# The first group of x loaded in two halves on two queues, and seven early products instead of nine

## The chip, the cores and the metric

The kernel runs on one core of one Trainium2 chip. The metric is device time in microseconds. Three runs of the kernel before gave 664.02, 663.25 and 662.78 us; the median is 663.25 us. The engines are TensorE (PE, with its weight loads as PEld), VectorE (DVE), ScalarE (ACT), GpSimd (POOL) and SyncE (SP). Transfers can be issued by SyncE, ScalarE and GpSimd, each with a queue of its own.

## The reference

Input x is (4, 2048, 256), all in 32-bit floats. Two layers follow one another, each with a residual sum and a layer norm after it:

```python
# attention without softmax, causal
q, k, v = (gelu(x @ W1 + b1) @ W2 + b2  for each of q, k, v)
scores = (q @ k.T) / sqrt(256 * 512) * tril(ones)
x = layernorm(x + (layernorm(scores @ v) * ln_w + ln_b))
# mixture of experts with soft slots: 16 experts of 16 slots
xn = layernorm(x) * gamma + beta
logits = unit(xn) * scale @ unit(mu)
dispatch, combine = softmax(logits over tokens), softmax(logits over slots)
slot_in = dispatch.T @ xn
slot_out = gelu(slot_in @ w1 + b1) @ w2 + b2        # per expert
x = layernorm(x + combine @ slot_out)
```

## The kernel before

**Tiling.** A group is W = 512 tokens (G = 4 blocks of 128 partitions by 256 channels); there are 16 groups, four to a batch element. For each group the kernel transposes x to channels by tokens (`xT`), makes the hidden layers of q, k and v (128x512 products with W1q, W1k, W1v at L802, each followed by ScalarE's Gelu at L812), and then k and v, the causal part, a running state, the norms and the logits. W2q and W2k are folded into one matrix at the start (`fold`, L728 on): both are transposed on TensorE (L738), copied by VectorE (L746), multiplied with one another (L760) and written by VectorE to `wqk_sb` (L770). The output of these three products goes through the three PSUM banks called `mm`, which the products of q, k and v use as well.

**Order.** Work is entered as steps with an engine, a length and what they read and write. A planner (`Plan`) lists the steps for each engine by expected times and ranks, and emits them in that order; each engine then runs its instructions in the order of emission. The framework adds semaphores for what depends on what, part by part of a tile. Loading is a step of the engine "SP" in the plan, whatever queue its transfers go to.

**Loading.** `load_x(t)` (L308) loads group t with one transfer of 512 KB on SyncE's queue (L315). For the first group it then calls `load_weights` (L370), which puts W1q, cols (the bias columns, 9 KB), W1v and W2q on ScalarE's queue in this order, W1k, W2k and W2v on SyncE's (256 KB each; L375 and L377), and mu, scale and two vectors on GpSimd's. After the second group's x comes `rows` (L387), 640 KB. Groups 0 and 1 are transposed on TensorE from x as loaded: `flips` (L479) puts four 128x128 transposes of one half of the channels into a bank (L486), first for half 0, then for half 1; `transpose_group` copies the first bank on VectorE (L476) and the second on ScalarE (L477). From group 2 on, x is loaded a second time as blocks of 32 by 32 in eight transfers of 64 KB (L338), which VectorE transposes in place (L787). For group 2 this comes on VectorE between the copies of the transposed W2q and W2k (L746) and those of the folded products (L770).

**Early products.** Before any data is there, TensorE multiplies the identity with itself (L461), nine times; each 32-bit product is two instructions in the profile. The results are not used.

Of the kernel before, what the change touches and what calls it, by code (L numbers as in the profile page):

```python
# [14 lines left out]
P = 128  # L15
G = 4
# [10 lines left out]
W = G * P  # L27
# [192 lines left out]
def kernel(  # L220
# [13 lines left out]
    nc = tc.nc  # L234
    B, T, C = x.shape
    E, _, H = w1.shape
# [71 lines left out]
    def load_x(t):  # L308
        if t >= ngroups:
            return  # L310
        b, g = divmod(t, NG)
        xt = plan.buffer("row", G)

        def emit():
            nc.sync.dma_start(  # L315
                out=xt[:, :, :C],
                in_=x[b, g * W : (g + 1) * W, :].rearrange("(c p) d -> p c d", p=P),
            )
            if t == 0:
                load_weights()  # L320
            if t == 1:
                load_rows()

        plan.step("SP", {0: 2.5, 1: 6.0, 2: 4.0}.get(t, 0.5), emit, writes=[xt])
        x_tiles[t] = xt
        if t < 2:
            return


        xs = plan.buffer("xT", KC)  # L330

        def emit_blocks():
            xb = x[b, g * W : (g + 1) * W, :].rearrange(
                "(n c) (k a r) -> a c k n r", c=32, k=KC, r=32
            )
            for a in range(P // 32):
                for k in range(KC):
                    nc.sync.dma_start(  # L338
                        out=xs[32 * a : 32 * (a + 1), k, :].rearrange(
                            "c (n r) -> c n r", r=32  # L340
                        ),
                        in_=xb[a][:, k],
                    )

        plan.step("SP", 4.8, emit_blocks, writes=[xs])
        xs_tiles[t] = xs
# [23 lines left out]
    def load_weights():  # L370
        for n, eng in (
            ("W1q", nc.scalar), ("W1k", nc.sync), ("W1v", nc.scalar),
            ("W2k", nc.sync), ("W2q", nc.scalar), ("W2v", nc.sync),
        ):
            eng.dma_start(out=wa[n], in_=w_attn[n].rearrange("(k p) d -> p k d", p=P))  # L375
            if n == "W1q":
                nc.scalar.dma_start(out=cols_sb, in_=cols)  # L377
        nc.gpsimd.dma_start(out=mu_sb, in_=mu.rearrange("(k p) e -> p k e", p=P))
        nc.gpsimd.dma_start(out=scale_sb, in_=scale.partition_broadcast(P))
        with nc.allow_non_contiguous_dma(reason="two vectors of one value a partition"):  # L380
            nc.gpsimd.dma_start(
                out=gb_sb.rearrange("p r k -> p (r k)"),
                in_=rows[3 * C : 5 * C].rearrange("(q p) -> p q", p=P),
            )

    def load_rows():
        nc.sync.dma_start(  # L387
            out=rows_sb.rearrange("p r d -> p (r d)"), in_=rows.partition_broadcast(P)
        )
# [31 lines left out]
    for n, after in (  # L421
# [29 lines left out]
        out=mask,  # L451
        in_=ones,
# [4 lines left out]
        channel_multiplier=-1,  # L457
    )

    for _ in range(9):  # L460
        nc.tensor.matmul(at_banks[0][:, :P], ident, ident, start=True, stop=True)  # L461

    hz_t = const.tile([P, NP, 2, S], F32, name="hz")
# [1106 lines left out]
    for t in range(ngroups):  # L1570
        b = t // NG
# [11 lines left out]
        if t == ngroups - 2:  # L1583
# [4 lines left out]
            cm, _ = softmaxes(early)  # L1588
            plan.begin(t + TAIL["part"])
            kept = part_sums(early)  # L1590
        if t % NG == NG - 1:
            groups = [t] if tail == 2 else list(range(t - NG + 1, t + 1))
            plan.begin(t + (TAIL["soft"] if tail == 2 else 1.4))
            _, less = softmaxes(groups, cm if tail == 2 else None)
# [52 lines left out]
```

## Time and profile before

| | us |
|---|---|
| median of the runs | 663.25 |
| the profiled execution | 663.13 |
| its span | 661.4 |
| TensorE busy | 647.2 (98%) |
| VectorE busy | 490.9 (74%) |
| GpSimd busy | 298.5 (45%) |
| ScalarE busy | 266.1 (40%) |
| first early product starts | 1.42 |
| first transpose of x starts | 5.64 |
| first product of q starts | 7.54 |
| first transpose of W2q starts | 11.08 |
| first product of v starts | 18.83 |

The page's first lines give each engine's busy time, its share of the span and its number of instructions. The chain of waits is followed back from the last instruction: each line has a start, a length, and what ran. A timeline line has start, length, engine, line, operation, and what it writes and reads; in brackets stands how long the engine stood idle before it and what ended that. "SPq" and "ACTq" are transfers issued by SyncE and ScalarE. In the lines on transfers, q1 is SyncE's queue, q10 ScalarE's and q0 GpSimd's, with packets, megabytes and the share of 16 transfer engines. The granted clock is 1.00 in all stretches up to 600 us.

### The profile page before, as it was taken

What the parts mean: (1) busy time and instruction counts of PE and PEld (TensorE: products, weight loads), DVE (VectorE), ACT (ScalarE), POOL (GpSimd) and SP (SyncE); (2) the same over time, 40 slices, a digit from 0 to 9 for tenths busy, and PEclk for the clock granted to TensorE, in tenths of its full rate; (3) what the DMA queues carried; (4) which work ended last, traced back from release to release, by engine and by line L of the source; (5) the groups of instructions that cost most, each with busy time, mean ns of one, the idle gap of its engine ahead of it and who ended that gap; (6) DMA issues with size and microseconds to landing.
All of it is one profiled execution on the core that took longest, in us unless ns stands there. A gap on an engine that the chain in (4) does not pass through costs nothing.

```text
span 661.4 us, 9366 instructions
## 1 busy us (share of the span) xinstructions
PE 647.2 (98%) x2972; PEld 483.3 (73%) x2972; DVE 490.9 (74%) x1294; ACT 266.1 (40%) x597; POOL 298.5 (45%) x346
## 2 busy tenths in 40 slices
PE   9999999999999999999999999999999999999995
PEld 6657586777768877758686887776767768887874
DVE  1438586979797878778796388996978489886486
ACT  3130515333346227221516323634153544545475
POOL 4343616060739514353426605546061937646234
PEclk9999999999999999999999999999999999999998
DMA  8953655777577095836676525994677372621274
GB/s 247 261 123 109 129 96 130 126 152 158 99 158 128 15 199 174 188 87 128 127 130 136 87 68 91 238 212 104 109 152 133 65 160 70 83 65 32 33 160 160
DMA packets 322233, 84.71 MB, mean 128 GB/s; under 512 B 253068, under 2 KB 319944, under 8 KB 322184
## 3 DMA queue, kind: packets, MB, share of 16 engines
q1 hardware_dynamic: 321080, 83.06, 59.7%
q10 hardware_dynamic: 960, 0.80, 0.4%
q8 instruction: 23, 0.38, 0.2%
q0 software_dynamic: 144, 0.26, 0.1%
q14 instruction: 26, 0.21, 0.1%
HBM read 52.05 MB, written 32.04 MB: 127 GB/s over the span
## 4 chain that ended last, share of the span: by engine, by line
PE 92%; DVE 5%; issue 1%; POOL 1%; POOLq 0%; ACT 0%; DVEq 0%; ACTq 0%
PE mm L802 25%; PE at L904 8%; PE mm L1171 8%; PE mm L852 8%; PE at L1316 8%; PE at L1542 7%; PE at L987 7%; PE mm L825 7%; PE at L877 4%; PE at L991 4%; PE at L937 1%; PE at L461 1%; PE tp L486 1%; DVE xn L1096 1%; PE mm L683 1%
## 5 line engine op out<-in xcount | busy, mean ns | idle before, releaser
L812 ACT ACTIVATE hid<-mm,cols_sb 128x512 f32<-128x512 f32 x96 | 65.1, 686 | 142.1 <-PE mm L802 141.5
L542 POOL TENSOR_TENSOR root<-ve,nhalf 128x4 f32<-128x4 f32 (+1 forms) x39 | 40.7, 1044 | 125.1 <-DVE ve L1037 51.2
L987 PE MATMUL at<-state,hid 128*128 128x256 f32 x240 | 61.6, 379 | 0.0
L904 PE MATMUL at<-vt,kt 128*128 128x256 f32 x240 | 61.3, 385 | 0.0
L825 PE MATMUL mm<-both_sb,hid 128*128 128x257 f32 x256 | 59.5, 381 | 1.4 <-DVE kt L835 1.4
L802 PE MATMUL mm<-xT,W1v_sb 128*128 128x512 f32 x128 | 59.5, 593 | 0.7 <-DVE both_sb L770 0.7
L802 PE MATMUL mm<-xT,W1q_sb 128*128 128x512 f32 x128 | 59.5, 595 | 0.3 <-DVE xT L476 0.3
L1542 PE MATMUL at<-so,ct 128*128 128x256 f32 x256 | 57.9, 381 | 0.8 <-DVE row L1550 0.6
L1316 PE MATMUL at<-row,lg 128*128 128x257 f32 x256 | 58.2, 380 | 0.0
L1171 PE MATMUL mm<-mu_sb,xnT 128*128 128x256 f32 x256 | 58.1, 379 | 0.0
L852 PE MATMUL mm<-W2v_sb,hid 128*128 128x256 f32 x256 | 58.0, 379 | 0.0
L802 PE MATMUL mm<-xT,W1k_sb 128*128 128x512 f32 x128 | 57.7, 593 | 0.0
L825 PEld LDWEIGHTS mm<-both_sb,hid 128*128 128x128 f32 x256 | 48.2, 190 | 9.7 <-DVE kt L835 2.0
L1542 PEld LDWEIGHTS at<-so,ct 128*128 128x128 f32 x256 | 48.0, 190 | 9.9 <-issue 1.7
L1171 PEld LDWEIGHTS mm<-mu_sb,xnT 128*128 128x128 f32 x256 | 48.4, 190 | 8.4 <-issue 1.5
L987 PEld LDWEIGHTS at<-state,hid 128*128 128x128 f32 x240 | 45.6, 190 | 11.8 <-issue 5.7
L1030 POOL TENSOR_TENSOR row<-row,rows_sb 128x1024 f32<-128x1024 f32 x16 | 35.0, 2186 | 42.4 <-DMA row<-in_x_dram 33.9
L852 PEld LDWEIGHTS mm<-W2v_sb,hid 128*128 128x128 f32 x256 | 48.5, 190 | 6.7
L1221 POOL TENSOR_TENSOR sum<-sum,ss 128x4 f32<-128x4 f32 x16 | 4.0, 248 | 109.4 <-DVE ss L1217 92.9
L1316 PEld LDWEIGHTS at<-row,lg 128*128 128x128 f32 x256 | 48.1, 190 | 7.2 <-issue 0.4
L904 PEld LDWEIGHTS at<-vt,kt 128*128 128x128 f32 x240 | 44.4, 190 | 12.0 <-issue 5.4
L946 ACT COPY cs<-at 128x256 f32<-128x256 f32 (+1 forms) x16 | 5.9, 371 | 109.1 <-PE at L937 97.5
(150 smaller groups left out, 1250.8 us busy)
## 6 DMA issues: line engine op xcount, KB each, us to landing
bounce<-xn SPq DMA_DIRECT2D x30, 512.0 KB
row<-in_x_dram SPq DMA_DIRECT2D x16, 512.0 KB
ct<-bounce SPq DMA_DIRECT2D x64, 128.0 KB
bounce<-kt SPq DMA_DIRECT2D x30, 256.0 KB
kT<-bounce SPq DMA_DIRECT2D x60, 128.0 KB
out_dram<-row SPq DMA_DIRECT2D x15, 512.0 KB
xT<-in_x_dram SPq DMA_DIRECT2D x112, 64.0 KB
xnT<-bounce SPq DMA_DIRECT2D x56, 128.0 KB
```

Source lines behind the costliest of these rows:

```text
L542: nc.gpsimd.tensor_tensor(r[:, :n], v[:, :n], nhalf.to_broadcast([P, n]), ALU.pow)
L802: nc.tensor.matmul(ph.place, wa[f"W1{n}"][:, k, m * P : (m + 1) * P], xT[:, k, :], start=(k == 0), stop=(k == KC - 1),)
L812: nc.scalar.activation(hid[n][:, m, :], ph.place, AF.Gelu, bias=cols_sb[:, 4 * i + m : 4 * i + m + 1],)
L825: nc.tensor.matmul(pk[:, : C + 1], hid["k"][:, k, c * P : (c + 1) * P], wqk_sb[:, k, :], start=(k == 0), stop=(k == KC - 1),)
L852: nc.tensor.matmul(pv[:, j * C : (j + 1) * C], hid["v"][:, k, (c0 + j) * P : (c0 + j + 1) * P], wa["W2v"][:, k, :], start=(k == 0), stop=( ...
L877: nc.tensor.matmul(psc[:, toks[c]], kT[:, k, toks[c]], qT[:, k, toks[c]], start=(k == 0), stop=(k == KC - 1),)
L904: nc.tensor.matmul(pds[:, m * C : (m + 1) * C], kt[:, c, m * P : (m + 1) * P], vt[:, c, :], start=True, stop=True,)
L987: nc.tensor.matmul(po[:, :C], qT[:, k, toks[c]], s[:, k, :], start=(k == 0), stop=False,)
L1030: lambda: nc.gpsimd.tensor_tensor(row[:, :, :C], row[:, :, :C], lnb_r, ALU.add),
L1171: nc.tensor.matmul(pl[:, j * ES : (j + 1) * ES], xnT[:, k, (c0 + j) * P : (c0 + j + 1) * P], mu_sb[:, k, :], start=(k == 0), stop=(k == KC ...
L1316: nc.tensor.matmul(psi[:, : C + 1], lg[:, c, h * P : (h + 1) * P], row[:, c, :], start=(i == 0), stop=(i == n - 1),)
L1542: nc.tensor.matmul(pc[:, :C], ct[:, h, c * P : (c + 1) * P], so_t[:, h, :], start=(h == 0), stop=(h == EH - 1),)
```

## The change

For the first group only, the load of x is two transfers of 256 KB: blocks 0 and 1 on SyncE's queue, blocks 2 and 3 on ScalarE's, both issued before the weights, so that W1q is second on ScalarE's queue. All other groups are loaded as before. Seven early products are issued instead of nine.

```diff
         def emit():
-            nc.sync.dma_start(
-                out=xt[:, :, :C],
-                in_=x[b, g * W : (g + 1) * W, :].rearrange("(c p) d -> p c d", p=P),
-            )
+
+            for i, eng in enumerate((nc.sync, nc.scalar) if t == 0 else (nc.sync,)):
+                n = G // 2 if t == 0 else G
+                cs = slice(i * n, (i + 1) * n)
+                eng.dma_start(
+                    out=xt[:, cs, :C],
+                    in_=x[b, g * W : (g + 1) * W, :].rearrange("(c p) d -> p c d", p=P)[:, cs],
+                )
             if t == 0:
                 load_weights()
...
-    for _ in range(9):
+    for _ in range(7):
         nc.tensor.matmul(at_banks[0][:, :P], ident, ident, start=True, stop=True)
```

## The prediction

> **What bounds the kernel now.** I read the page first, then the chain of waits for the first 40 us, because the change touches nothing later, then the timeline and the transfers of the first 20 us.
>
> ```profile
> span 661.4 us, 9366 instructions
> ...
> PE 647.2 (98%) x2972; PEld 483.3 (73%) x2972; DVE 490.9 (74%) x1294; ACT 266.1 (40%) x597; POOL 298.5 (45%) x346
> ```
>
> TensorE (PE) is busy 98% of the span, so only its few idle places can be won or lost. The chain of the start (start us, length us, what):
>
> ```profile
> 1.42 4.21 PE at L461 x18
> ...
> 5.64 1.92 PE tp L486 x8
> 7.56 3.69 PE mm L802 x8
> 11.24 0.87 PE tp L738 x8
> 12.12 3.43 PE mm L802 x8
> 15.55 2.62 PE mm L760 x12
> ...
> 18.39 0.40 DVE both_sb L770
> ...
> 18.83 3.70 PE mm L802 x8
> ```
>
> Nine early products are 18 instructions (L461). Then come x's transposes (L486), the q products (L802), the transposes of W2q and W2k (L738), the k products, and the folded weight (L760). Up to 18.2 us the chain is TensorE alone; then, for one step, it is VectorE (DVE). The timeline shows what each step stood waiting for:
>
> ```profile
> 5.33 0.37 SPq L315 DMA_DIRECT2D row<-in_x_dram  x1
> 5.64 1.57 PEld L486 LDWEIGHTS tp<-ident,row 128*128 128x128 f32 x8 [0.31 <-DMA row<-in_x_dram]
> ...
> 5.74 0.54 SPq L387 DMA_DIRECT2D rows_sb<-in_rows_dram  x1
> ...
> 10.97 0.91 PEld L738 LDWEIGHTS tp<-ident,both_sb 128*128 128x128 f32 x8 [0.56 <-DMA both_sb<-in_W2q_dram]
> ...
> 17.22 1.25 DVE L787 STREAM_TRANSPOSE xT<-xT 128x1024 f32<-128x1024 f32 x1 [4.14 <-DMA xT<-in_x_dram]
> ...
> 18.39 1.05 DVE L770 TENSOR_SCALAR both_sb<-mm 128x257 f32<-128x257 f32 x3
> ...
> 18.83 1.55 PE L802 MATMUL mm<-xT,W1v_sb 128*128 128x512 f32 x3 [0.67 <-DVE both_sb L770]
> ```
>
> Three waits matter. x lands just as the early products end (5.6 us). W2q lands at 10.93 us by its semaphore events, and its first weight load goes out at 10.97, so W2q is just in time. And DVE stands at L787 until the third group's xT has landed (17.14 us); only then does it empty the first folded bank (L770), whose bank the v products need. TensorE waits 0.67 us for that. Transfers up to 4.75 us (packets, MB):
>
> ```profile
> q1 hardware_dynamic: 444, 0.45, 29.0%
> q10 hardware_dynamic: 266, 0.26, 21.4%
> ```
>
> q1 is SyncE's queue (x first), q10 is ScalarE's (W1q first). Both are in flight together, and ScalarE's first 256 KB (256 packets) are through by about 4.8 us.
>
> **The change, part by part.**
>
> *Two early products fewer.* Each is two instructions, 18 in 4.21 us, 0.213 us apart. Four of them are 0.85 us; TensorE is free at 4.78 instead of 5.63 us, and could take a transpose at 4.57. Whether that is worth anything hangs on x.
>
> *x in halves.* SyncE's half is 256 packets. q1 had sent its 256th at 3.8 us and its 512th at 4.93; x's semaphore was full at 5.60. The half should be seen by about 4.5. ScalarE's half stands where W1q stood: W1q's 256 packets were out at 4.8 and it was seen at 5.31. So I take 5.31 for it (not before 4.9, if q10 starts sooner behind a shorter x; not after 5.60). Halves of a tile are waited for one by one: the q products start on xT's first half at 7.54 and take the second at 8.23, "0.39 <-ACT xT L477". So two transposes run before 5.31; the third and fourth end at 5.97, DVE's copy (0.69 us, L476) ends at 6.7, and the q products could start at 6.73 instead of 7.54.
>
> *W1q second on its queue.* From 4.85 us both queues share about 365 GB/s, as from 4.5 to 5.5 us now. Half of it takes 1.4 us for 256 KB, plus the 0.5 us from W1q's last packet to its semaphore now: 6.75 to 6.95 us. The q products then start at about 6.85, 0.7 us sooner, and end at 10.4.
>
> *W2q, last on ScalarE's queue.* It now stands behind 256 KB more. After W1q come cols (a gap of 0.35 us and 0.45 us of small packets, as now), so W1v starts at about 7.05 instead of 5.9 us: some 165 packets behind by what q10 moved in that time. Late in the queue (9 to 10 us) q10 moved 173 packets per us, so W2q lands 0.9 us later, at 11.83. TensorE is in order and takes W2q before the k products: done at 10.4, it waits 1.4 us, and what was won is lost. L738 starts 0.9 us later than now. Bounds: nothing later, if q10 fills its gaps; 2.7 us later, if all 256 extra packets went at the 95 per us of 7 to 9 us, when POOL's queue takes a share. I take 0.9, since the last stretch decides.
>
> *The v products.* The folded weight would end at 18.17 + 0.9 = 19.07. The v products start at the later of that and DVE's L770, 18.83 if xT lands as now. The cost is 0.9 - 0.67 = 0.23 us. VectorE's order hides the rest. L770 needs the first folded bank at 18.39, and this is ready near 17.3 (first folded product 15.39 + 0.9, plus four instructions).
>
> *xT's landing.* All queues share one set of engines, 90% or more busy from 3.5 to 13 us, and the bytes up to xT are the same; what q10 carries more, q1 carries less. SyncE's issue is also held by eight semaphores in rotation: it issued the second x at 5.33 when W1q had landed (5.31), rows at 5.74 after x (5.60). One transfer more moves the waits by one: x's second group then waits for a half of x, rows for W1q (6.9). The fifth xT piece now starts to issue at 11.31 and is held until 13.47 with rows and four pieces outstanding; an earlier wait moves inside that. I take 0. Bounds: 0.4 us sooner, if the thin stretch from 2.6 to 3.6 us (about 150 GB/s) fills; 0.9 us later, if it followed W2q.
>
> *Issue slots.* ScalarE issues one transfer more ahead of W1q: 0.5 us (L375 and L377: 0.46 to 0.52). W1q goes out at 1.30, cols 1.83, W1v 2.36, W2q 2.87. Nine transfers on eight semaphores also hold the last until the first lands, at worst W2q until 5.3, with ScalarE's table load (1.28 us) behind it until 7.1. The copy of xT's second half could run at 6.8, so 0.3 us; W2q's own lateness covers it, and it would count in full without that. W2q's packets are not due before 9 us. Held on SyncE instead, W2v goes out about 5 us with W2k still ahead of it. POOL's three transfers keep their place (2.12 us).
>
> *The sum.* Start -0.7, W2q's wait +1.6 (0.7 won and 0.9 lost), slack -0.67, xT 0: +0.2 us on the profiled execution of 663.13 (span 661.4, and 1.7 around it) makes 663.35. The median of the runs, 663.25, is 0.12 above the profiled one: 663.5.
>
> A rule to weigh: the row first, q1 and q10 each moved about 0.09 MB from 4.0 to 4.5 us. The Trainium skill, DMA: Bandwidth & Descriptors, section "Issuing engines are not separate DMA queues", says that transfers of all issuers interleave on the same engines and that issuing from several saves issue time only. By it alone, W1q and W2q pay for whatever x gains; the sum by the rule would be no gain, as mine.
>
> **Rivals.** *The start's gain passes through.* For it: x is seen 0.3 us sooner, and 0.85 us of filler goes. Against it: W2q already ends a wait now, and DVE's xT wait ends last at 18.8. It needs W2q no later and xT 0.5 to 0.8 us sooner: 662.9 to 662.6.
>
> *W2q later still.* At 1.5 to 2.7 us the cost is 0.8 to 2.0: 664.1 to 665.3. For it: the thin rates of q10 from 7 to 9 us. Against: most of W2q moves after 9.
>
> *TensorE's clock rises later (the slower side).* Transposes at 5.64 to 7.19 us still run 0.213 us apart, those of L738 0.109: full speed came between 7.19 and 7.54, some 5.9 us after the first product. Now TensorE may stand idle up to 0.5 us before x's second half. If that starts the count anew at 5.31, full speed comes at 11.2; the q products run 0.84 us apart (0.429 doubled, as the transposes' spacing is) instead of 0.429 and end near 12.5. L738 is then 1.4 us late, +0.7: 664.2. If the wait for W1q resets it too, full speed comes at 12.8 and it is +1.5: 665.0. It decides once L738 is over 0.67 us late. Against it: the gap is short, and the granted clock says 1.00 throughout, which doesn't show this.
>
> The Trainium skill, TensorE: Matmul & The Clock Gate, Part 1, has a free-running window of about 3.4 us for this and asks for 4 us of steady work, which speaks against fewer products; by its window the clock rival would cost about 0.5 us as an estimate, and differ from run to run. The 5.9 us of this trace is longer than either figure.
>
> **Chances.** W2q takes the gain and slack hides most: 0.55, itself 663.1 to 664.0. Gain passes: 0.18. W2q later still: 0.13. Clock: 0.14. I call within 0.2% (1.33 us, 661.9 to 664.6) no change, about what a measurement of this kernel can tell; the runs before span 662.78 to 664.02. Over 664.6 lie about half of the clock case and a third of the W2q case: 0.11. Under 661.9 lies a fifth of the gain case: 0.04. So 0.04, 0.85, 0.11. The range is 662.5 to 664.8.
>
> **What would show it.** Right: SyncE's half seen by 4.6 and ScalarE's near 5.3 us; q products near 6.9; an idle of over 1 us before L738 put down to W2q's transfer, landing near 11.8; L787 still near 17.2, the v products at 18.8 to 19.1. Wrong: L738 before 11.1 and L787 before 16.8 (gain passes); q products 0.84 us apart (clock); L787 after 17.6, which I price at nothing.

## The result, and the profile after

The changed kernel's median is 664.28 us, that of the kernel before in the same comparison 662.51 us (17 runs of each). The ratio is 1.0028, with a 95% interval of 1.0016 to 1.0041: a little slower, by 1.1 to 2.7 us. The time lies inside the range of the prediction (662.5 to 664.8) and 0.8 us above the predicted 663.5. The same two programs were compared once more (experiment 5), and the ratio there was smaller, 1.0013 (1.0002 to 1.0023).

The profiled executions are 663.13 us (span 661.4) before and 664.11 us (span 662.4) after, so these two traces hold 0.98 us of the difference. The page of the kernel after, the same lines as in the prediction:

```profile
span 662.4 us, 9361 instructions
...
PE 646.8 (98%) x2968; PEld 482.0 (73%) x2968; DVE 491.1 (74%) x1294; ACT 266.1 (40%) x597; POOL 298.6 (45%) x346
```

TensorE works 0.4 us less (four instructions of 0.21 us are gone, and such totals vary by a microsecond: 647.2 and 646.2 in two traces of the kernel before), and the span is 1.0 us longer. So it is waits that were added. The chain of waits of the kernel after, for the start of the span (start us, length us, what). Line numbers are 4 higher than before: L465 is the early products, L490 the transposes of x, L742 those of W2q and W2k, L764 the folded products, L774 their writing out, L791 VectorE's transposition of xT, L806 the products of q, k and v.

```profile
0.79 3.55 DMA row<-in_x_dram
...
4.36 7.17 DMA both_sb<-in_W2q_dram
...
11.58 1.09 PE tp L742 x8
12.67 3.44 PE mm L806 x8
16.10 2.62 PE mm L764 x12
...
18.80 0.40 DVE both_sb L774
...
19.24 3.70 PE mm L806 x8
```

Before, this chain was TensorE alone from 1.42 to 18.2 us. Now it is a transfer up to 11.53 us: W2q, whose issue on ScalarE's queue at 4.36 us follows on the landing of x's first transfer there (4.33). The late issue can hardly be what makes W2q late: W1v, ahead of it on the queue, landed only at 10.03. What TensorE does ahead of 11.53 is off the path. The timeline of the same execution (in brackets: idle time before, and what ended it):

```profile
4.56 1.91 PE L490 MATMUL tp<-ident,row 128*128 128x128 f32 x8
...
6.40 3.72 PE L806 MATMUL mm<-xT,W1q_sb 128*128 128x512 f32 x8
...
11.58 1.09 PE L742 MATMUL tp<-ident,both_sb 128*128 128x128 f32 x8 [1.45 <-DMA both_sb<-in_W2q_dram]
...
17.63 1.25 DVE L791 STREAM_TRANSPOSE xT<-xT 128x1024 f32<-128x1024 f32 x1 [4.00 <-DMA xT<-in_x_dram]
...
18.80 1.05 DVE L774 TENSOR_SCALAR both_sb<-mm 128x257 f32<-128x257 f32 x3
...
19.24 3.70 PE L806 MATMUL mm<-xT,W1v_sb 128*128 128x512 f32 x8 [0.53 <-DVE both_sb L774]
```

The reader sees the early gain and where it goes. x's transposes start 1.08 us sooner than before (5.64 to 4.56) and the q products 1.14 us sooner (7.54 to 6.40). Then TensorE stands 1.45 us for W2q, and L742 starts 0.5 us later than before (11.08 to 11.58). The folded products end at 18.72 instead of 18.17. The v products wait beyond that, as before, for VectorE, which takes up L791 only when the third group's xT has landed: 17.45 us by its semaphore events, 17.14 before. They start 0.41 us later. Of that 0.31 is the landing. The other 0.10 is VectorE's own checking: it checks the semaphores of xT's eight pieces in a fixed order, and starts 0.18 us after the last landing now, 0.08 before, as the last piece is on a semaphore that is checked third instead of fourth.

The rest of the 0.98 us comes afterwards. TensorE's last product ends 0.62 us later (653.77 to 654.39), so that 0.21 us was added in the middle. From that product to the span's end it is 8.00 us instead of 7.64, another 0.36. SyncE's own waits at the end of the span (us in total, times, longest), before and then after:

```profile
SPq L1640 <- DMA out_dram<-row: 2.5, 3, 1.0
```

```profile
SPq L1644 <- DMA out_dram<-row: 2.9, 1, 2.9
```

SyncE's transfers and ScalarE's signal their ends on eight semaphores in rotation, and the last thing that SyncE does is to check all eight in a fixed order. With one transfer more, the last store falls on another of the eight. Before, it was the one checked last: three waits, 2.5 us in all, and the other checks were done while the store was under way. After, it is the one checked first: one wait of 2.9 us, and the other six checks come behind it, 0.06 us apart. From the landing of the last store to the span's end it is 0.90 us before and 1.26 after.

### The profile page after: what moved, and what is told of

The parts are those of the page before. It is cut to its first block, busy times and chain, and to the rows that moved or that the text cites. A ratio compares the mean times of both kernels' runs of the same rounds, so it can differ in the third digit from the quotient of the medians.

```text
span 662.4 us, 9361 instructions
## 1 busy us (share of the span) xinstructions
PE 646.8 (98%) x2968; PEld 482.0 (73%) x2968; DVE 491.1 (74%) x1294; ACT 266.1 (40%) x597; POOL 298.6 (45%) x346
## 4 chain that ended last, share of the span: by engine, by line
PE 91%; DVE 5%; DMA 2%; issue 1%; POOL 0%; POOLq 0%; ACT 0%; DVEq 0%; ACTq 0%
PE mm L806 24%; PE at L908 8%; PE mm L1175 8%; PE mm L856 8%; PE at L1320 8%; PE at L1546 7%; PE at L991 7%; PE mm L829 7%; PE at L881 4%; PE at L995 4%; PE at L941 1%; DMA both_sb<-in_W2q_dram 1%; DMA row<-in_x_dram 1%; DVE xn L1100 1%; PE mm L687 1%
## 5 line engine op out<-in xcount | busy, mean ns | idle before, releaser
L806 PE MATMUL mm<-xT,W1v_sb 128*128 128x512 f32 x128 | 59.5, 593 | 0.5 <-DVE both_sb L774 0.5
L806 PE MATMUL mm<-xT,W1q_sb 128*128 128x512 f32 x128 | 59.5, 595 | 0.3 <-DVE xT L480 0.3
L806 PE MATMUL mm<-xT,W1k_sb 128*128 128x512 f32 x128 | 57.6, 593 | 0.0
```

The source lines that it names most:

```text
L806: nc.tensor.matmul(ph.place, wa[f"W1{n}"][:, k, m * P : (m + 1) * P], xT[:, k, :], start=(k == 0), stop=(k == KC - 1),)
```

## The experiments

Theory A: the loss is in transfers; one of two landings sets the v products, W2q's (0.6 us later) or that of the third group's xT (0.3 later). Theory B: TensorE's clock, which comes to full speed later with less early work or with gaps. Beside them stand the end of the span, and whatever differs later. Each ratio is to the kernel before, run on the same chip at the same time.

**1. The two halves, with nine early products.** Part of the change alone.

```diff
-    for _ in range(7):
+    for _ in range(9):
```

> The split with nine early products instead of seven. Theory A (transfers): the loss of the changed kernel comes from W2q and the third group's xT landing later behind the split, so two more early products change nothing: the q products start near 7.3 us instead of 6.4, TensorE's wait for W2q shrinks from 1.45 to 0.6 us, W2q lands at 11.5 and the v products start at 19.2 as in the changed kernel; the time stays 1.4 to 2 us over the kernel before (ratio 1.002 to 1.003). Theory B (clock): the gap after seven products holds TensorE's clock down in many executions, and with nine the time is back within 0.4 us of the kernel before.

Ratio 1.0014 (1.0005 to 1.0023), span 662.3. The transposes start at 4.90 instead of 4.56, the q products at 6.28 (not near 7.3, as I had expected: the spacing of products halved at 4.3 us in this trace), W2q lands at 11.64, for which TensorE waits 1.71 us, xT at 17.60, and the v products start at 19.40. The two products fewer are worth nothing here: at 4.9 us TensorE is ahead of W2q by more than it can use, with seven or nine.

**2. Seven early products, x whole.** The other part alone, on the kernel before.

```diff
-    for _ in range(9):
+    for _ in range(7):
```

> Seven early products with x unsplit, as in the kernel before. Theory A (transfers): TensorE stands idle for 0.8 us until x lands at 5.6 us, the transfers are those of the kernel before, the v products start at 18.8 us, and the time is that of the kernel before (ratio 0.9994 to 1.0006). Theory B (clock): products of q run 0.84 us apart for some us, and the time is 0.7 to 1.8 us longer (ratio 1.001 to 1.003).

Ratio 1.0012 (0.9999 to 1.0024), span 662.0. The timeline of this kernel:

```profile
5.83 1.97 PE L486 MATMUL tp<-ident,row 128*128 128x128 f32 x8 [1.05 <-DMA row<-in_x_dram]
...
7.73 5.12 PE L802 MATMUL mm<-xT,W1q_sb 128*128 128x512 f32 x8
12.68 1.04 PE L738 MATMUL tp<-ident,both_sb 128*128 128x128 f32 x8
```

Here theory B's effect is real: TensorE stands 1.05 us, and the eight q products take 5.12 us instead of 3.70, since the spacing halves only at 10.6 us, where it did so at 7.4 in the kernel before. L738 is 1.60 us late and the v products, at 19.60, are 0.77 us late. In the changed kernel x comes sooner and this does not happen: its spacing halves at 6.5 us, at 6.9 in the second trace of it.

**3. W2q ahead of W1v on ScalarE's queue**, in the changed kernel.

```diff
-            ("W1q", nc.scalar), ("W1k", nc.sync), ("W1v", nc.scalar),
-            ("W2k", nc.sync), ("W2q", nc.scalar), ("W2v", nc.sync),
+            ("W1q", nc.scalar), ("W1k", nc.sync), ("W2q", nc.scalar),
+            ("W2k", nc.sync), ("W1v", nc.scalar), ("W2v", nc.sync),
```

> The changed kernel with W2q ahead of W1v on ScalarE's queue. Both theories of which landing costs: if it is W2q's (my prediction's step), L738's transposes start near 10.2 us without an idle place, and the time falls by 0.4 us or more against the changed kernel. If it is the landing of the third group's xT, which the profiled pair suggests (17.45 against 17.14 us), the transposes are early all the same, but the v products still start at 19.2 us and the time stays that of the changed kernel (ratio to the kernel before 1.002 to 1.003).

Ratio 1.0044 (1.0026 to 1.0061), span 665.5: slower still. The timeline:

```profile
10.92 1.09 PE L742 MATMUL tp<-ident,both_sb 128*128 128x128 f32 x8 [0.65 <-DMA both_sb<-in_W2q_dram]
...
18.72 1.25 DVE L791 STREAM_TRANSPOSE xT<-xT 128x1024 f32<-128x1024 f32 x1 [5.75 <-DMA xT<-in_x_dram]
...
20.33 5.40 PE L806 MATMUL mm<-xT,W1v_sb 128*128 128x512 f32 x8 [2.28 <-DVE both_sb L774]
```

W2q came 0.66 us sooner, and L742 is back where it was before the change. The v products start 1.09 us later than in the changed kernel. So W2q's lateness isn't what sets them: xT is, which landed at 18.54, 1.1 us later. The exchange moved which transfer each piece of xT has to wait for before it is issued (the fourth waits for W2q, until 10.87 us; the fifth is held until 14.92). And after the wait of 2.28 us the v products take 5.40 us instead of 3.70; this run's granted clock is 0.50 from 20.4 to 23.8 us.

**4. rows later.** In the changed kernel `rows` (640 KB, between the second x and xT on SyncE's queue) is loaded after the third group's xT.

```diff
-            if t == 1:
-                load_rows()
...
+            if t == 2:
+                load_rows()
```

> The changed kernel with rows (640 KB) loaded after the third group's xT instead of before. If xT's landing sets the v products, it lands up to 1.9 us sooner (640 KB at about 340 GB/s), VectorE no longer ends the wait, and the v products start at 18.75 us, which W2q sets: 0.5 us sooner than in the changed kernel, ratio to the kernel before 1.001 to 1.002. If W2q's landing alone set them, or if the loss lies later in the kernel, the time stays at 1.002 to 1.003.

The lines of TensorE and VectorE:

```profile
11.76 1.09 PE L742 MATMUL tp<-ident,both_sb 128*128 128x128 f32 x8 [1.65 <-DMA both_sb<-in_W2q_dram]
...
15.64 1.25 DVE L791 STREAM_TRANSPOSE xT<-xT 128x1024 f32<-128x1024 f32 x1 [1.83 <-DMA xT<-in_x_dram]
...
17.86 1.03 PE L764 MATMUL mm<-row,cols_sb 128*128 128x257 f32 x4
...
18.73 3.60 PE L806 MATMUL mm<-xT,W1v_sb 128*128 128x512 f32 x8
```

With xT 1.9 us sooner there is no wait before the v products: they follow the folded products at 18.73, 0.51 us sooner than in the changed kernel and 0.10 before the kernel before. Here W2q alone sets them. In the changed kernel itself it is xT. The end still has the 0.36 us (7.98 from TensorE's last product), and the span is 661.7, 0.3 above the kernel before. The ratio, 1.0015 (1.0002 to 1.0028), isn't lower than the changed kernel's second one, so half a microsecond at the start can't be seen in these medians.

**5. and 6. Both kernels again, unchanged.** To learn how much a trace and a median vary.

> The changed kernel once more, beside other runs of the kernel before, with a second trace. Theory A (the loss is the landing of W2q and of the third group's xT, 0.4 us by the first pair of traces): ratio 1.0005 to 1.0015, and the v products start at 19.0 to 19.5 us. Theory B (TensorE's clock: its waits of 1.5 us and more let the clock fall, or rise late, in part of the executions, 1.7 us each time): ratio 1.002 to 1.004, with the times in two clusters about 1.7 us apart.

> The kernel before under another name, against itself: ratio 1.000 with the interval across it, whatever the theory. Its trace shows how much moves without any change: theory A has the v products at 18.8 us within 0.2; theory B has the instant at which TensorE reaches full speed anywhere between 4 and 7.6 us (7.4 in the first trace).

The kernel after again: ratio 1.0013 (1.0002 to 1.0023). The kernel before against itself: 1.0007 (0.9996 to 1.0018). The times of the kernel after lie spread from 662.46 to 664.93, without the two clusters of theory B. The second pair of traces has spans of 662.9 and 661.3, 1.6 us apart where the first pair has 1.0. The start: W2q lands at the same 11.53 us, 0.66 later than in its partner, xT at 17.87 against 17.08, the v products start 0.89 us later. The lines of VectorE and TensorE, the kernel before and then the kernel after:

```profile
17.16 1.25 DVE L787 STREAM_TRANSPOSE xT<-xT 128x1024 f32<-128x1024 f32 x1 [4.20 <-DMA xT<-in_x_dram]
...
18.77 3.70 PE L802 MATMUL mm<-xT,W1v_sb 128*128 128x512 f32 x8 [0.72 <-DVE both_sb L770]
```

```profile
18.05 1.25 DVE L791 STREAM_TRANSPOSE xT<-xT 128x1024 f32<-128x1024 f32 x1 [4.42 <-DMA xT<-in_x_dram]
...
19.66 3.70 PE L806 MATMUL mm<-xT,W1v_sb 128*128 128x512 f32 x8 [0.95 <-DVE both_sb L774]
```

TensorE's last product is 1.26 us later, and the end adds 0.34. So three pieces recur (W2q 0.6 to 0.7, xT 0.3 to 0.8, end 0.34 to 0.36), and a fourth, in the middle, is 0.21 in the one pair and 0.37 in the other. There the traces drift apart and together again near 285 us and between 430 and 460 us, where waits of about 1 us are there in some executions and not in others, and whether any of it belongs to the change isn't settled.

**7. rows later in the kernel before.** The same diff as in 4, on the kernel before.

> The kernel before with rows loaded after the third group's xT. If that xT's landing holds the v products in the kernel before too, TensorE's wait of 0.67 us there goes, the v products start at 18.2 us, and the time falls by 0.6 us (ratio 0.999). If not, ratio 1.000.

Ratio 0.9983 (0.9971 to 0.9996), a little faster: xT lands at 15.64 and the v products start at 18.01 with no wait, 0.82 us sooner. The span of the one trace, 661.2, is only 0.2 shorter: the rest is lost again further on, and this trace doesn't show where the 1.1 us of the ratio come from.

**8. rows later, and W1k exchanged with W2q**, in the changed kernel.

```diff
-            ("W1q", nc.scalar), ("W1k", nc.sync), ("W1v", nc.scalar),
-            ("W2k", nc.sync), ("W2q", nc.scalar), ("W2v", nc.sync),
+            ("W1q", nc.scalar), ("W2k", nc.sync), ("W1k", nc.scalar),
+            ("W2q", nc.sync), ("W1v", nc.scalar), ("W2v", nc.sync),
```

> The changed kernel with two edits: rows after the third group's xT, and W1k and W2q exchanged between the two queues (SyncE: half of x, W2k, W2q, W2v; ScalarE: half of x, W1q, cols, W1k, W1v). If the wait for W2q is what took the start's gain, L738's transposes follow the q products at 10.1 us without an idle place, the v products start near 17.3 us, 1.4 us sooner than with rows alone moved, and the time is 1 to 1.5 us under the kernel before (ratio 0.998). If the loss lies elsewhere, the ratio stays at 1.001 or over.

Ratio 0.9968 (0.9955 to 0.9981), the fastest of all. TensorE:

```profile
10.25 1.04 PE L742 MATMUL tp<-ident,both_sb 128*128 128x128 f32 x8
...
17.55 3.70 PE L806 MATMUL mm<-xT,W1v_sb 128*128 128x512 f32 x8 [0.23 <-DVE both_sb L774]
```

Nothing waits for W2q any more. The q products start 1.13 us sooner than in the kernel before (6.41), the v products 1.28: nothing takes the start's gain away again, and most of the wait ahead of the v products (0.67 us) has gone too. But 0.82 of the 1.28 us is what 7 won without the change. The halves of x and the exchange add 0.46 at the v products (18.01 to 17.55) and cost 0.36 at the end, and the intervals of 7 and 8 overlap; so it isn't shown that the early x is worth its time. The kernel before with both edits and x whole was not run. The whole ratio (2.1 us) is more than that. In this trace two later waits of 1.38 and 0.98 us, near 59 and 285 us, are absent, which are there in the kernel before.

**9. The exchange of W1k and W2q without rows.**

> The changed kernel with only W1k and W2q exchanged between the queues; rows stay ahead of the third group's xT. W2q then lands before 10 us, L738's transposes follow the q products without an idle place and the folded weight ends near 17.4 us. If W2q's landing sets the cost of the change, the v products start at 18.8 us or sooner and the time is that of the kernel before or less (ratio under 1.0005). If VectorE's wait for the third group's xT sets it, the v products still start at 19.2 to 19.7 us, TensorE waits some 1.8 us there instead of 0.5 to 0.95, and the ratio stays at 1.001 to 1.002.

Ratio 1.0044 (1.0026 to 1.0061), which I had not expected to be as slow as that. The timeline:

```profile
9.95 1.04 PE L742 MATMUL tp<-ident,both_sb 128*128 128x128 f32 x8
...
16.00 1.03 PE L764 MATMUL mm<-row,cols_sb 128*128 128x257 f32 x4
19.67 5.40 PE L806 MATMUL mm<-xT,W1v_sb 128*128 128x512 f32 x8 [2.65 <-DVE both_sb L774]
```

W2q is off the path (L742 at 9.95, the folded products done at 17.03), and the v products still start at 19.67, because xT lands at 17.88. The exchange made xT 0.43 us later as well, so this run alone doesn't separate the two landings, but all the traces together do: in all eleven in which the v products wait, they start 1.64 to 1.80 us after xT's landing, wherever W2q's was (6.77 to 11.64). This run also shows a second price. The stretches of this trace (us, busy time of PE, PEld, DVE, ACT and POOL, granted clock, share of the transfer engines, GB/s):

```profile
17.00:20.00 3.00, 0.35 (x2) 0.30 (x2) 1.94 (x4) 0.00 (x0) 0.13 (x1) 1.00 0.95 306
20.00:23.40 3.40, 3.40 (x5) 1.35 (x4) 0.28 (x1) 0.16 (x1) 3.40 (x3) 0.50 1.07 291
23.40:26.00 2.60, 2.60 (x10) 1.53 (x9) 0.02 (x1) 1.21 (x2) 2.60 (x3) 1.00 1.11 215
```

After 2.65 us without a product the clock is granted at 0.50 for 3.4 us. The eight v products take 5.40 us, 1.7 more than at full speed. That, the start's 0.84 us and the end's 0.36 are 2.9 of the 3.9 us by which this span is longer than that of the kernel before.

**10. One transfer more, late.** In the kernel before, the store of group 8 goes out in two transfers, to test the end alone.

```diff
-            nc.sync.dma_start(
-                out=out[b, g * W + c0 * P : g * W + (c0 + n) * P, :].rearrange(
-                    "(c p) d -> p c d", p=P
-                ),
-                in_=row[:, c0 : c0 + n, :C],
-            )
+            for k, m in ((c0, n),) if t != 8 else ((c0, n // 2), (c0 + n // 2, n // 2)):
+                nc.sync.dma_start(
+                    out=out[b, g * W + k * P : g * W + (k + m) * P, :].rearrange(
+                        "(c p) d -> p c d", p=P
+                    ),
+                    in_=row[:, k : k + m, :C],
+                )
```

> The kernel before with the output of group 8 stored in two transfers instead of one, in the middle of the kernel: one transfer more, as in the changed kernel, and nothing else. If the 0.36 us that the changed kernel loses after TensorE's last product comes from SyncE checking eight transfer semaphores in a fixed order at the end (the last store sits on the first of them instead of the last), the stretch from TensorE's last product to the end of the span is 8.0 us instead of 7.65. If it comes from the loading at the start, it stays at 7.65.

One execution, 664.61 us, span 662.9. SyncE's waits at the end:

```profile
SPq L1641 <- DMA out_dram<-row: 2.4, 1, 2.4
```

One wait, as in the changed kernel, and from the landing of the last store to the end 1.27 us instead of 0.90: one transfer more, with nothing changed at the start, has the later end of 0.36 us. But the whole from TensorE's last product is 7.55 us, not the 8.0 that this would give, because the store itself landed 2.80 us after its issue instead of 3.26. The order of the checks is confirmed, the sum of the end isn't. In all the traces of this case the landing-to-end time falls into two groups: 0.90 to 0.92 us in the kernel before (twice) and in 2, 7 and 11, and 1.26 to 1.27 in every kernel with one transfer more on these two queues. This trace's xT landed at 17.40 and its v products started at 19.09, though nothing was changed there: such a landing varies by some 0.3 us by itself. In the four traces with x whole and rows in its place xT lands at 17.03 to 17.40, in the three with x in halves and the weights in their order (the kernel after twice, and 1) at 17.45 to 17.87.

**11. cols on GpSimd's queue**, on top of 8, so that SyncE and ScalarE issue as many transfers as before the change.

```diff
-                nc.scalar.dma_start(out=cols_sb, in_=cols)
+                nc.gpsimd.dma_start(out=cols_sb, in_=cols)
```

> Rows moved and W1k and W2q exchanged, as in the fastest kernel so far, and cols loaded on GpSimd's queue ahead of mu. The transfers that share the eight semaphores are then as many as in the kernel before, so the last 0.36 us come back (7.65 us after TensorE's last product), and W1v no longer waits behind cols. Ratio to the kernel before 0.996 to 0.997. Against it: mu is issued 0.6 to 1 us later, which would show as GpSimd starting mu's squares after 10 us, with no cost expected.

Ratio 0.9984 (0.9970 to 0.9999). The end is back at 0.92 us after the last landing and 7.66 after the last product, as before the change. Another thing that differs is a stretch from 7.6 to 8.4 us in which the kernel after moves few bytes (cols' own small packets pass before it, from 5.2 to 6.8 us). That stretch in the kernel after, and then in this one:

```profile
7.60:8.40 0.80, 0.80 (x3) 0.34 (x2) 0.00 (x0) 0.80 (x1) 0.00 (x0) 1.00 0.53 176
```

```profile
7.60:8.40 0.80, 0.80 (x3) 0.35 (x2) 0.00 (x0) 0.07 (x1) 0.00 (x0) 1.00 1.10 368
```

The kernel before has 335 GB/s there, so the changed kernel moves 0.13 MB less in this time (159 GB/s by 0.8 us), which at 365 GB/s is 0.35 us, about what xT is late in the first pair. That fits, but it isn't shown to be the cause: in the second pair the stretch lacks less (207 GB/s against 315, 0.09 MB) and xT was later by more, 0.79 us; with the stretch filled, xT still came no sooner than in 8 (L791 at 16.14 instead of 15.94), and 10 had xT late with a full stretch. Although the end was 0.36 us shorter, the kernel isn't faster than 8, and the ratio isn't the 0.996 to 0.997 that I expected.

**12. Kernel 8 again.**

> The fastest kernel so far once more (rows after the third group's xT, W1k and W2q exchanged). If the early start of the v products (17.55 us, 1.3 us sooner than in the kernel before) is what it wins, less 0.36 us at the end, the ratio is 0.998 to 0.999 and TensorE's waits near 59 and 285 us (1.4 and 1.0 us), which its first trace lacked, are back. If those waits go because the start is earlier, they are away again and the ratio is 0.996 to 0.997.

Ratio 0.9980 (0.9966 to 0.9994). The v products start at 17.71 after 0.76 us of waiting, and the two later waits are partly back (0.47 and 1.01 us). So 8 is faster than the kernel before on two chips, by 0.2 to 0.3%: about 1.1 us of it are the start's, less 0.36 at the end, and the rest are later waits that come and go. Against kernel 7, which has rows moved and x whole (0.9983), no gain is shown.

## Why the prediction was right or wrong

**x in halves: too late by a microsecond.** I had 4.5 us for SyncE's half and 5.31 for ScalarE's; they were seen at 4.02 and 4.33 (4.22 and 4.54 in the second trace). I had put ScalarE's half where W1q stood. But its queue began to send at 2.4 us instead of 2.65, and from 2.8 to 3.6 us the two halves moved 350 GB/s where before there were 169. The transfers up to 4.75 us, after (packets, MB, share of 16 transfer engines):

```profile
q1 hardware_dynamic: 514, 0.50, 34.7%
q10 hardware_dynamic: 383, 0.38, 23.1%
```

ScalarE's queue had sent 117 packets more than before by that time, SyncE's 70 more. The thin stretch filled, which I had only as a bound for xT, and it was x that gained. The Trainium skill, DMA: Bandwidth & Descriptors, section "Issuing engines are not separate DMA queues", which I had weighed, speaks of a saving in issue time only; here x landed 1.3 us sooner (5.60 to 4.33), more than an issue, which took 0.4 to 0.5 us. A good half of that needs no faster transfers, only the new order: before, the two queues together had sent 514 packets by 4.25 us, about the 512 that x has, but 182 of them were W1q's, and x's own last one went at 4.96. After, x's last one went at 3.77, and by 3.75 both had sent 552. Where the rest comes from was not tested apart. The rule and this trace agree further on: what x gained, W2q paid for.

**No gap after seven products.** I let TensorE stand up to 0.5 us for the second half; the transposes follow at 4.56 without one. The q products start at 6.40, not 6.85, and the gain at the start is 1.1 us, not 0.7.

**W2q: right in kind, too large in size.** I had +0.9 us, to 11.83; it was +0.6, to 11.53 in both traces. TensorE's wait, 1.45 us, is the 1.4 I named, which is luck: both its start (10.12 for 10.4) and its end (11.53 for 11.83) came 0.3 us sooner. L742 was 0.5 us late and the folded products ended within the 0.67 us of slack that I counted, at 18.72, so that W2q cost nothing against the kernel before; experiments 3 and 9, which brought it sooner (and xT later), won nothing.

**xT's landing: "I take 0" is the step that failed.** It landed 0.31 us later in the first pair and 0.79 in the second, and that is what the v products waited for. L791 at 17.63 and 18.05 is past the 17.6 that I had named as a sign of being wrong, and the v products, at 19.24 and 19.66, are past the 19.1 that I had named as the latest if I was right. My slack of 0.67 us was slack against W2q only, since the same xT had made it. Experiment 4 takes xT off the path, and the v products start 0.51 us sooner; 9 takes W2q off, and they start 1.79 us after xT's landing, as in the kernel after. That xT waits for landings of other transfers is seen in 3, where the order of the weights alone moved it by 1.1 us. Why it moved by 0.3 to 0.8 us here is open: in the first pair rows and the fifth piece were issued 0.2 to 0.3 us later (fifth piece released at 13.76 instead of 13.47), but in the second the fifth was released 0.02 us later and the last issued 0.02 later, so there the time went after the issue. The thin stretch fits in size in the first pair alone, and 10 and 11 don't bear it out.

**The end: a term that I did not have.** I counted the ninth transfer on eight semaphores only where it holds an issue at the start. It also shifts the rotation for the rest of the kernel, and both SyncE at the end and VectorE ahead of L791 check their semaphores in a fixed order: 0.36 us from the last landing to the end, in every kernel with one transfer more, and 0.10 us between xT's landing and L791 in both pairs. Over all fourteen traces that second delay is 0.18 us with xT's last piece on the semaphore checked third, 0.08 on the fourth, 0.02 on the last.

**The sum.** Predicted +0.2 us on the profiled execution. Measured +0.98: 0.41 at the v products (I had 0.23 there), 0.36 at the end, 0.21 in between. In the second pair 1.60: 0.89, 0.34 and 0.37. The medians differ by 1.77 in the one comparison and by 0.88 in the other, so the traces account for the difference within what it varies, no more closely than that. That 664.28 lies in the range is partly luck: the kernel before measured 662.51 beside it, 0.74 below the 663.25 that I reckoned from, and the difference was 1.77 us, where I had 0.25.

**The rivals.** "The gain passes through" fell: W2q ends the first part of the path, xT the next. "W2q later still" fell: 0.6, not 1.5. The clock rival fell for this change: the spacing of products halved at 6.5 and 6.9 us, against 7.4 and 4.7 in the kernel before. Its effect exists, though (a late rise in 2, a drop in 3 and 9), and the seven early products would have brought it on had x not come sooner. I had priced it at 0.7 to 1.5 for the v products; in 2 it was 0.77.

**The chances.** I gave 0.85 to no change within 0.2%, 0.11 to slower. The ratio's interval, 1.0016 to 1.0041, lies mostly beyond 0.2%, in the second comparison mostly within it. Slower deserved much more: both terms that I left at nothing, xT's landing and the end, cost 0.3 us or more.

## What to carry to other kernels

At the start of a kernel whose loads share the transfer engines, bringing one load forward pays only up to the next load that something waits for; list the landings in the order in which the critical engine needs them, and ask which one ends the wait after the one that you removed. Slack before a wait covers a delay only if what makes that wait is not itself moved by the change: two waits that end close together must be taken away together (8 took both out of the change, 3, 4 and 9 one). Compare such a repair with the old kernel repaired alike: of the 1.28 us that 8 won at the v products, 7 has 0.82 without the change. And a transfer more or less is never only that one transfer: with a fixed number of completion semaphores in rotation it moves what each later issue waits for, and which semaphore of a set is checked last.

## What was not expected of the hardware

- *Where the last transfer falls among the eight semaphores is worth 0.36 us.* Landing to end is 0.90 to 0.92 us where the last store is checked last, and 1.26 to 1.27 where it is checked first, in fourteen traces.
- *A wait of 2.3 us cost more than its length.* After 2.28 and 2.65 us of waiting TensorE's clock went to 0.50 for 3.4 us, which added 1.7 us to eight products; after 1.45 to 1.71 us it did not. The Trainium skill, TensorE: Matmul & The Clock Gate, Part 1, puts the return to half speed after at least one idle window of about 3.4 us. The length of the drop here is that window's; the idle time that brought it on was shorter. In the clock's record of all fourteen traces, each stretch at full speed is a whole multiple of 3.41 us long (13.65 us, four times, in 3 and 9).
- *Full speed comes at no fixed time.* The spacing halves at 7.4 and 4.7 us in two traces of the same kernel before, at 7.1 and 5.3 in two of kernel 8. The page's free-running window would make it so.
- *VectorE is stretched beside GpSimd.* In the kernel before, one operation of VectorE with two inputs from memory takes 0.48 us alone and 1.83 beside an addition of GpSimd's:

```profile
53.27 0.48 DVE L1014 SCALAR_TENSOR_TENSOR a<-a,mv,rows_sb 128x256 f32<-128x256 f32 x1
...
54.62 2.18 POOL L1030 TENSOR_TENSOR row<-row,rows_sb 128x1024 f32<-128x1024 f32 x1 [6.62 <-DMA row<-in_x_dram]
...
55.26 1.83 DVE L1014 SCALAR_TENSOR_TENSOR a<-a,mv,rows_sb 128x256 f32<-128x256 f32 x1
```

It ends at 57.09, 0.29 us after GpSimd's addition (56.80). In this trace all five that began while such an addition ran ended 0.28 to 0.29 us after it. The later waits of about 1 us go with this: the one near 285 us is missing in just two of the fourteen traces (the second of the kernel before, the first of kernel 8), and in just these two no such operation between 275 and 282 us is stretched (0.47 to 0.48 us, against one of 2.0 to 2.5 in each of the others). That the one makes the other was not tested.
